# Sorting the tokens of a 32-expert FFN: one block behind an attention, or chunk by chunk within it

## The chip, the cores and the metric

The kernel runs on one core of a Trainium2 chip. The metric is the device time of one execution in microseconds (us); several executions are made and the median is taken. The core has TensorE (PE; its weight loads are listed as PEld), VectorE (DVE), ScalarE (ACT), GpSimd (POOL) and SyncE (SP, which here only issues DMAs). Each engine works through its own instructions in order.

## The reference: what is computed

A decoder of four layers over x of 128 x 64 tokens of width 128. Each layer is an attention-like block, a cross attention with a context, and an FFN, each added to x and followed by a layernorm. The change concerns layer 1, whose cross attention is causal (16 heads of width 8) and whose FFN picks one of 32 experts for each token:

```python
x = _layernorm(x + _L1_xattn_ref(x, ctx_1024, ctx_1024, ...))   # causal
x = _layernorm(x + _L1_ffn_ref(x, router_w, router_b, weights1, bias1, weights2, bias2))
```

The kernel computes that FFN as: the logits are x times the 128 x 32 router weights plus a bias; the expert with the largest logit (the first of equals) is e; y = relu(relu(x W1[e] + b1[e]) W2[e] + b2[e]), with 32 hidden units per expert.

## The kernel before

The 8192 tokens are 16 chunks of 512 (four tiles of 128). X[c] holds chunk c in SBUF throughout. The steps at the end of the kernel run one after the other: ..., attn_diff, xattn_causal, ffn_routed, attn_alibi, ....

**The attention helper** (`attention`, L1171 to L1387) is a software pipeline. Pass c does the second half of chunk c-1's values, the weights of chunk c, the scores of chunk c+1 and the projections of chunk c+2, in four parts k = 0 to 3; at the end of each it calls `aside(c, k, seen)`, with the last instructions so far (`seen`), behind which an aside can queue its own. Maxima of the scores are reductions on DVE (L1260), the exponentials run on ACT (L1309), the values are 64 small products (L1327, av_ps) and DVE normalises them (L1332, L1341). Score and weight tiles (`wide`) take turns in five PSUM banks, everything else (`bank`) in three. POOL does part of the head expansion (L1202) and applies the layernorm (L387). The causal attention passes no aside. The alibi attention behind the FFN does: its aside gathers the routed outputs back. The attention with the key mask (layer 3) does too: its aside sorts for the last FFN, mostly one chunk's transposes and logits a pass.

**The routed FFN** (`ffn_routed`, L1663) treats chunks 10 to 15 as dense and 0 to 9 as routed.

- Dense: all 32 experts at once. `choose` (L1682) transposes a chunk and makes logits and the one-hot choice, `spread` (L1691) turns the choice into a mask, `hidden` (L1702) makes 8 x 512 hidden rows in two halves of four products, a mask product and four Relus on ACT (L1714), `output` (L1717) sums over them tile by tile (L1724, L1725), and a layernorm follows. `hidden` and `output` call `between` before each half and each tile.
- Routed: `plan` (L1749) sorts the 40 tiles of 128 tokens by expert. For all ten chunks it makes transposes and logits (L1756, L1759) into one 40 x 32 table, then the one-hot choices over the whole table (DVE instructions of 1280 elements), prefix products with a triangle and with ones (L1781, L1782), counts rounded up to 128, one running sum over 1312 elements (L1793), and the positions. Then 40 indirect DMAs from POOL (L1805) write each tile's rows to their places in an array XR in HBM.
- Quads: 18 groups of four sorted tiles. `fetch` (L1818) has SP read four expert numbers and issue eight weight loads; `rows` (L1832) loads the quad's rows from XR through ACT's DMA queue (L1834); `turn` (L1836) transposes them, `inner` (L1844) and `outer` (L1852) make the two layers, and SP stores the result (L1865) from one of four buffers. `rejoined` (L1906) gathers the results within the alibi attention.

The order is written out at L1874 to L1904: the eleven logit steps of the plan, choose and spread of the first dense chunk, then the dense chunks with the rest of the plan's steps between them, `fetch` for 13 quads, three `rows`, and the quads one after the other. The plan's big tables lie in the two VX tiles and two tiles of the tag "e", which the attention uses as well. A list scheduler orders instructions at build time by readiness and by the order of tracing; `issue_after` makes it keep an instruction behind another of the same engine.

Of the kernel before, what the change touches and what calls it, by code (L numbers as in the profile page):

```python
# [12 lines left out]
F32 = mybir.dt.float32  # L13
# [227 lines left out]
def tile_decoder(ctx: ExitStack, tc: tile.TileContext, a, out):  # L241
# [1274 lines left out]
    def causal_steps():  # L1516
        w = W[4]
        return attention(
            cross(w, None, None), w[:, 2, :],
            lambda c, s: out_projected(c, s["o"], w[:, 3, :], bv=col("l1xbv"), base=lambda: with_bias(c, "l1xbo")),  # L1520
            mask=everywhere(half[:, 128:256].rearrange("p (n h k) -> p n h k", n=2, h=1)), late_laid=True,
        )
# [140 lines left out]
    def ffn_routed():  # L1663
        w = W[5]
        both, spare = work("tab", (P, 1024), "selb2"), work("tab", (P, 1024), "wqs")
# [5 lines left out]
        rest, whole = work("tmp", (P, D), "b2rest"), both[:, P : 2 * P].bitcast(BF16).rearrange("p (n m) -> p n m", n=2)  # L1671
        b2, part = whole[:, 0], whole[:, 1]
# [9 lines left out]
        def choose(c):  # L1682
            xT = transposed(X[c], "xT")
            full = (P, TPC, E32)
            l = logits(xT, col("l1fr"), E32, row("l1frb"), "lg32", work("t1", full, "lg32"))
            oh, _ = first_of(l, E32, "rev32", [P, TPC], "rt", work("tmp", full, "rt_s"), work("o", full, "rt_o"))
# [15 lines left out]
        def hidden(c, between):  # L1702
            xT, _, ohm = st[c]
            hT = work("h", (P, 8, 512), "hT8")
            for n in range(2):
# [6 lines left out]
                for j in range(4):  # L1712
                    k = 4 * n + j
                    A.activation(hT[:, k, :], ps[j], AF.Relu, bias=col("l1fb1")[:, k : k + 1])  # L1714
# [16 lines left out]
        T, NE, W_ = TPC * len(ROUTED), E32, TPC * len(ROUTED) * E32  # L1731
        span = NE * (T + 1)
        first, second = work("e", (P, 2048), "plan"), work("e", (P, 2048), "plan")
        LG, same = (t[:, :W_].rearrange("p (t e) -> p t e", t=T) for t in (first, second))
        ahead = first[:, :span].rearrange("p (e t) -> p e t", e=NE)
        inside = second[:, :W_].rearrange("p (e t) -> p e t", e=NE)
        each = VX[0][:, :span].rearrange("p (e t) -> p e t", e=NE)
        oh = VX[0][:, span : span + W_ // 2].bitcast(BF16).rearrange("p (t e) -> p t e", t=T)
        keep = VX[1][:, :span].rearrange("p (e t) -> p e t", e=NE)
        o = span  # L1740
        sums, o = VX[1][:, o : o + 4 * NE].rearrange("p (k e) -> p k e", k=4), o + 4 * NE
        halves, o = VX[1][:, o : o + P].bitcast(BF16).rearrange("p (k m) -> p k m", k=2), o + P
        pos, o = VX[1][:, o : o + T], o + T
        whole, o = VX[1][:, o : o + NE].bitcast(I32), o + NE
        whose, o = VX[1][:, o : o + P].bitcast(I32), o + P
        gf = VX[1][:, o : o + 1]
        where = RT["where"] = sm.tile([P, 40], I32, tag="pli0", name="pli", bufs=1)[:, :T]

        def plan():  # L1749
            V.tensor_copy(halves, sq[:, 1:3, :])  # L1750
            G.memset(keep, 1.0)
            G.memset(keep[:, :, 0:1], 0.0)
            behind = None
            for i in [*range(len(ROUTED)), None]:
                if i is not None:
                    xT = transposed(X[ROUTED[i]], "tmp")  # L1756
                if behind:
                    k, x = behind
                    logits(x, col("l1fr"), E32, row("l1frb"), "lg32", LG[:, k * TPC : (k + 1) * TPC, :])  # L1759
                behind = (i, xT) if i is not None else None  # L1760
                yield
            m = sm.tile([P, TMAX, 1], F32, tag="fo_m", name="p1_m")[:, :T]
            yield from first_of_steps(LG, E32, "rev32", [P, T], "rp", same, oh, m)
            V.tensor_reduce(sums[:, 0], oh.rearrange("p t e -> p e t"), AX.X, ALU.add)
            ps = bank("cnt_ps")
            mm(ps[:, :NE], sq[:, 2, :], sums[:, 0], start=True, stop=True)
            V.tensor_scalar(sums[:, 1], ps[:, :NE], float(P - 1), None, ALU.add)
            yield
            V.tensor_copy(whole, sums[:, 1])
            V.tensor_single_scalar(whole, whole, 7, ALU.logical_shift_right)  # L1770
            V.tensor_copy(sums[:, 1], whole)
            V.tensor_tensor_scan(sums[:, 2], sc("iota")[:, 1:2].to_broadcast([P, NE]), sums[:, 1], 0.0, ALU.mult, ALU.add)
            V.tensor_tensor(sums[:, 3], sums[:, 2], sums[:, 1], ALU.subtract)
            V.tensor_scalar(each[:, :, 0], sums[:, 3], float(P), None, ALU.mult)
            yield
            flat = oh.rearrange("p t e -> p (t e)")
            for k in range(0, T, 16):
                n = min(16, T - k)
                q = slice(k * NE, (k + n) * NE)
                inn, tot = wide("in_ps"), wide("tot_ps")  # L1780
                mm(inn[:, : n * NE], halves[:, 0, :], flat[:, q], start=True, stop=True)  # L1781
                mm(tot[:, : n * NE], halves[:, 1, :], flat[:, q], start=True, stop=True)  # L1782
                A.copy(inside[:, :, k : k + n], inn[:, : n * NE].rearrange("p (t e) -> p e t", t=n))
                A.copy(each[:, :, 1 + k : 1 + k + n], tot[:, : n * NE].rearrange("p (t e) -> p e t", t=n))
                yield
# [83 lines left out]
        def take(n):  # L1869
            for _ in range(n):  # L1870
                with tc.issue_after(RT["dve"].ins) if "dve" in RT else nullcontext():
                    next(planned, None)
# [427 lines left out]
```

## Time and profile before

| | us |
|---|---|
| median of 6 runs | 3144.7 (3131.98 to 3153.53) |
| the profiled execution, its time | 3152.46 |
| its span, first to last instruction | 3150.5 |
| PE busy | 2782.6 (88%) |
| DVE busy | 2008.3 (64%) |
| ACT busy | 1643.4 (52%) |
| POOL busy | 1520.8 (48%) |
| mean granted PE clock | 0.940 |

The profile records one execution. A stretch's row gives its length, each engine's busy time and the PE clock granted, as a share of the full clock. A timeline row gives start, duration, engine, line, operation, output and inputs, shapes and how many such instructions were merged; in brackets stands how long the engine idled before and on what it waited. The chain of waits follows the work that ended last back to what released it; its rows are start, duration and line. All times in the prediction count from the span's start; the causal attention's full passes lie between about 1060 and 1300, the routed FFN's stage between 1326 and 1535.

### The profile page before, as it was taken

The page shows a single profiled execution, that of the slowest core. Times are in us where ns is not written, and L with a number is a line of the kernel's source. Part 1 is how long each engine was busy: PE and PEld are TensorE (multiplying, and loading weights), DVE is VectorE, ACT ScalarE, POOL GpSimd, SP SyncE. Part 2 cuts the span into 40 slices and gives each one's busy share as a digit, 9 for nine tenths or more (in the row PEclk, how much of TensorE's full clock was granted, in tenths as well). Part 3 has the DMA queues.
Part 4 walks back from the last instruction along what each step waited for, and adds up shares of the span by engine and source line. Part 5 has one row for each costly group of instructions (what it writes and reads, how often), then busy time and mean ns, then how long its engine had stood idle before and what let it go on. Part 6 is the DMA issues. An engine that isn't in the chain of part 4 may idle for free.

```text
span 3150.5 us, 110712 instructions
## 1 busy us (share of the span) xinstructions
PE 2782.6 (88%) x46690; PEld 2046.0 (65%) x46690; DVE 2008.3 (64%) x7278; ACT 1643.4 (52%) x3376; POOL 1520.8 (48%) x1521
## 2 busy tenths in 40 slices
PE   5899989999999899998899999989898679998993
PEld 3789856656666677865577767764443347766882
DVE  3743469667777666553477656667878776674355
ACT  3444457754554565432366555644555666654453
POOL 3566556144555444325277435556666123444344
PEclk9999989999999999889899989999998889998997
DMA  4578821000000200003611000000000000011683
GB/s 129 151 202 260 253 62 43 6 8 3 3 3 7 69 4 4 7 19 99 178 19 18 4 6 4 4 12 1 1 1 11 1 12 19 17 32 61 213 254 117
DMA packets 191634, 182.23 MB, mean 58 GB/s; under 512 B 30176, under 2 KB 166624, under 8 KB 191136
## 3 DMA queue, kind: packets, MB, share of 16 engines
q1 hardware_dynamic: 160688, 136.66, 14.6%
q0 software_dynamic: 20224, 32.28, 4.2%
q8 instruction: 366, 6.00, 0.7%
q10 hardware_dynamic: 10224, 6.22, 0.7%
q14 instruction: 132, 1.08, 0.1%
HBM read 132.34 MB, written 42.73 MB: 56 GB/s over the span
## 4 chain that ended last, share of the span: by engine, by line
PE 55%; DVE 25%; POOL 5%; ACT 5%; issue 5%; DMA 4%; SPq 1%; POOLq 0%; ACTq 0%; DVEq 0%
PE av_ps L1327 9%; DVE m L1260 7%; PE s_ps L1252 5%; PE h_ps L790 5%; PE yg L803 5%; PE t_ps L1290 4%; DMA got<-l_rout,fat 2%; PE v_ps L1229 2%; PE xT_ps L332 2%; PE t_ps L1302 2%; POOL x L387 2%; PE ye_ps L2027 1%; PE y L1134 1%; PE y L1724 1%; DVE lnst L373 1%
## 5 line engine op out<-in xcount | busy, mean ns | idle before, releaser
L1260 DVE TENSOR_REDUCE m<-s_ps 128x8 f32<-128x512 f32 x640 | 397.4, 683 | 117.5 <-PE s_ps L1648 41.2
L1309 ACT ACTIVATE e<-t_ps 128x512 f32<-128x512 f32 x640 | 329.9, 602 | 150.8 <-PE t_ps L1302 150.4
L1327 PE MATMUL av_ps<-vx,e 128*64 128x18 f32 (+1 forms) x10240 | 336.4, 215 | 10.7 <-issue 5.6
L1327 PEld LDWEIGHTS av_ps<-vx,e 128*64 128x64 f32 x10240 | 318.2, 139 | 30.8 <-issue 23.1
L792 ACT ACTIVATE hT<-h_ps,aux 128x256 f32<-128x256 f32 x496 | 206.6, 469 | 221.5 <-issue 112.1
L1290 PE MATMUL t_ps<-eb,kT 32*64 32x128 f32 x10240 | 284.3, 287 | 6.9 <-DVE m L1260 2.4
L1202 POOL TENSOR_SCALAR eb<-qT,small 128x512 f32<-128x512 f32 x75 | 124.5, 1661 | 329.3 <-ACT qT L972 177.6
L825 POOL DMA_INDIRECT got<-l_rout,fat x192 | 193.7, 1009 | 174.4 <-DVE r L835 68.2
L790 PE MATMUL h_ps<-ebT,rw 128*128 128x256 f32 x992 | 242.4, 389 | 14.0 <-DVE ebT L778 8.8
L1290 PEld LDWEIGHTS t_ps<-eb,kT 32*64 32x64 f32 x10240 | 200.6, 133 | 74.6 <-DVE m L1260 25.4
L803 PEld LDWEIGHTS yg<-rw,hT 128*128 128x128 f32 x1984 | 241.0, 192 | 6.3
L803 PE MATMUL yg<-rw,hT 128*128 128x128 f32 x1984 | 241.3, 275 | 0.0
L387 POOL TENSOR_SCALAR x<-xb,lnmv,ln_y 128x128 f32<-128x128 f32 x200 | 157.2, 798 | 170.6 <-DVE ln_y L352 167.8
L1252 PE MATMUL s_ps<-eb,qT 32*64 32x256 f32 x5120 | 218.3, 399 | 16.3 <-DVE m L1260 9.7
L765 POOL DMA_INDIRECT aux<-in_x_dram,rat x156 | 159.7, 1024 | 113.3 <-PE h_ps L790 48.7
L1332 DVE RECIPROCAL rc<-av_ps 128x32 f32<-128x32 f32 (+1 forms) x192 | 61.4, 320 | 235.4 <-PE av_ps L1327 235.1
L790 PEld LDWEIGHTS h_ps<-ebT,rw 128*128 128x128 f32 x992 | 182.8, 194 | 39.2 <-DVE ebT L778 13.6
L804 DVE TENSOR_TENSOR yo<-yg,aux 128x256 f32<-128x256 f32 x124 | 52.3, 422 | 239.7 <-PE yg L803 239.5
L1200 ACT ACTIVATE eb<-qT,small 128x512 f32<-128x512 f32 x160 | 106.9, 714 | 122.6 <-POOL qT L1434 118.0
L1252 PEld LDWEIGHTS s_ps<-eb,qT 32*64 32x64 f32 x5120 | 113.8, 134 | 57.3 <-DVE m L1260 12.7
L1202 POOL TENSOR_SCALAR eb<-kT,small 128x512 f32<-128x512 f32 x75 | 136.0, 1813 | 19.3 <-ACT kT L972 10.6
L2027 PE MATMUL ye_ps<-w_l2f,box 128*128 128x512 f32 x256 | 135.2, 653 | 0.0
(525 smaller groups left out, 6381.8 us busy)
## 6 DMA issues: line engine op xcount, KB each, us to landing
rw<-in_l0w_dram SPq DMA_DIRECT2D x78, 512.0 KB
rw<-in_l3w_dram SPq DMA_DIRECT2D x46, 512.0 KB
l_rout<-yo SPq DMA_DIRECT2D x124, 128.0 KB
aux<-xd SPq DMA_DIRECT2D x46, 128.0 KB
aux<-in_l0b_dram SPq DMA_DIRECT2D x78, 66.0 KB
xd<-vx SPq DMA_DIRECT2D x5, 1024.0 KB
plan<-xr ACTq DMA_DIRECT2D x18, 256.0 KB
x<-in_x_dram SPq DMA_DIRECT2D x16, 256.0 KB
```

Source lines behind the costliest of these rows:

```text
L387: (V if on_dve else G).tensor_scalar(X[c][:, t, :], r[:, t, :], mv[:, t, 0:1], y[:, t : t + 1], ALU.subtract, ALU.mult)
L790: s.pe = mm(ps[:, j * GR : (j + 1) * GR], w1[:, (k + j) * P : (k + j + 1) * P], ebT, start=True, stop=True)
L792: s.act_ins = A.activation(hT[k + j], ps[:, j * GR : (j + 1) * GR], s.act, bias=v[:, k + j : k + j + 1])
L803: s.pe = mm(y[:, i * P : (i + 1) * P], hT[k][:, i * P : (i + 1) * P], w2[:, k, :], start=(k == 0), stop=(k == FK - 1))
L825: s.gather = G.indirect_dma_start(out=got[i][k][:, t, :], out_offset=None, in_=s.rout[b][:, :], in_offset=bass.IndirectOffsetOnAxis(ap=at[ ...
L1202: ins = (G if h == 2 and not early else V).tensor_scalar(dst, x, mine, None, ALU.mult)
L1252: mm(ps[g][j * S : (j + 1) * S, u * 256 : (u + 1) * 256].rearrange("p (h k) -> p h k", h=4), rows32(s["q"], g)[:, b], rows32(s["eb"], g)[: ...
L1260: last = V.tensor_reduce(s["m"][:, g, 2 * hf : 2 * hf + 2, :].rearrange("p t h -> p (t h)"), ps[g].rearrange("p (n k) -> p n k", k=S), AX. ...
L1290: mm(ps[g][i * S : (i + 1) * S].rearrange("p (a u j q) -> p a u j q", u=2, a=2, j=2)[:, :, u, j, :], rows32(s["k"], g)[:, b], rows32(s["eb ...
L1309: last = A.activation(e[:, g, :], ps[g], AF.Exp, scale=scale)
L1327: mm(av[j * S : (j + 1) * S, 8 * (u - u0) + n, :], ev[:, n // 2, n % 2, u, j, :], vx[:, 2 * (2 * hf + u) + j, n, :], start=True, stop=True,)
L2027: mm(ps[k].rearrange("p (e d) -> p e d", e=4), s["x1T"][n][:, t * P : (t + 1) * P], w[0][:, 4 * k : 4 * k + 4, :], start=True, stop=False, ...
```

## The change

The plan becomes a sequence of small steps for one chunk each, and it starts within the causal attention, as its aside `presort`.

- In pass c = 2 the FFN's preamble runs. From there one plan step is taken at k = 0 and k = 2 of each pass, and from (12, 3) on at every k. Chunk i's `chosen` (logits, one-hot choice, and a running count `before` of the choices per expert in the tiles ahead) is in pass i+3 at k = 0; `ranked` (two bfloat16 products of width 128 that give each token's rank among its expert's, and a product and a reduction on DVE) at k = 2 together with the transposes of the next chunk. Passes 12 and 13 make the counts, the experts' starts and the positions; passes 14 to 16 take twelve scatter steps of two tiles. `choose` and `spread` of the first dense chunk are in pass 16.
- The large tables, the running sum over 1312 elements and the copies of the prefix products go. The plan now keeps one tile of the tag "tab" and two of "t1".
- After the attention SP fetches weights for 13 quads at once. The scatter steps left are taken among the first two dense chunks, two at each `between`.
- The quads' steps are no longer behind the dense chunks: from the third chunk's output on, each `between` of `output` takes one, and from the fourth chunk on the first half of `hidden` too. Rows are loaded behind the latest Relu on ACT.

```diff
+            aside=lambda c, k, seen: presort(c, k, seen),
...
+        def turned(i):
+            st["x"] = transposed(X[ROUTED[i]], "tmp")
+
+        def chosen(i):
+            mine = oh[:, i * TPC : (i + 1) * TPC]
+            logits(st["x"], col("l1fr"), E32, row("l1frb"), "lg32", l)
+            m = sm.tile([P, TMAX, 1], F32, tag="fo_m", name="p1_m")[:, :TPC]
+            for _ in first_of_steps(l, E32, "rev32", [P, TPC], "rp", same, mine, m):
+                pass
+            for t in range(TPC):
+                z, n = divmod((i * TPC + t + 1) % (2 * TPC), TPC)
+                V.tensor_tensor(before[:, z, n], before[:, i % 2, t], mine[:, t], ALU.add)
+
+        def ranked(i):
+            q = slice(i * TPC, (i + 1) * TPC)
+            mine = oh[:, q]
+            ps = bank("rk_ps")[:, : TPC * NE]
+            mm(ps, halves[:, 0, :], mine.rearrange("p t e -> p (t e)"), start=True, stop=False)
+            mm(ps, halves[:, 1, :], before[:, i % 2].rearrange("p t e -> p (t e)"), start=False, stop=True)
+            V.tensor_tensor(same, mine, ps.rearrange("p (t e) -> p t e", t=TPC), ALU.mult)
+            V.tensor_reduce(rank[:, q], same, AX.X, ALU.add)
...
+            for i in range(n):
+                chosen(i)
                 yield
+                ranked(i)
+                if i + 1 < n:
+                    turned(i + 1)
+                yield
...
+            for k in range(0, T, 2 * TPC):
+                q = slice(k, k + 2 * TPC)
+                V.tensor_tensor(two, oh[:, q], sums[:, 0, None, :].to_broadcast([P, 2 * TPC, NE]), ALU.mult)
+                V.tensor_reduce(pos[:, : 2 * TPC], two, AX.X, ALU.add)
+                V.tensor_tensor(rank[:, q], rank[:, q], pos[:, : 2 * TPC], ALU.add)
+                if k in (0, 4 * TPC):
+                    yield
+            V.tensor_copy(where, rank)
...
+        def rows(q):
+            eb[q] = S_["first"][:, q % 4 * 512 : (q % 4 + 1) * 512].rearrange("p (i d) -> p i d", i=4)
+            with tc.issue_after(RT["act"].ins):
+                nc.scalar.dma_start(out=eb[q], in_=XR[q * 4 * P : (q + 1) * 4 * P, :].rearrange("(i p) d -> p i d", p=P))
...
+        def quads(near):
+            for q in range(3):
+                rows(q)
+            for q in range(QUADS + 2):
+                if 0 <= q - 2:
+                    outer(q - 2)
+                if q > 2 and q - 3 + near < QUADS:
+                    fetch(q - 3 + near)
+                if q + 3 < QUADS:
+                    rows(q + 3)
+                if q < QUADS:
+                    turn(q)
+                if 0 <= q - 1 < QUADS:
+                    inner(q - 1)
+                yield
...
+        def presort(c, k, seen):
+            if c < 2:
+                return
+            with ExitStack() as behind:
+                for i in seen:
+                    if i:
+                        behind.enter_context(tc.issue_after(i))
+                if k in (0, 2) or (c, k) >= (12, 3):
+                    next(planned, None)
+            if c == NC and k == 0:
+                choose(d0)
+            elif c == NC and k == 2:
+                spread(d0)
...
+        near = homes()
+        for q in range(near):
+            fetch(q)
...
-            hT = hidden(c, lambda n: take(1 if k else 0))
+            hT = hidden(c, lambda n: take(2) if k < 2 else next(quad, None) if k > 2 and n == 0 else None)
...
-            output(c, hT, lambda t: take(2 if k == t == 0 else 1 if k == 0 or t % 2 else 0))
+            output(c, hT, lambda t: take(2) if k < 2 else next(quad, None))
```

## The prediction

> **What bounds the kernel now.** I read the page's slices first: TensorE is busy 88% of the span, so the useful question is where it is idle or slow. Then the table by stretches, for the attention that the sort is moved into and for the routed FFN behind it. Columns: stretch, its length, busy time of PE, PEld, DVE, ACT and POOL with the number of instructions, granted PE clock, DMA share, GB/s.
>
> ```profile
> 1075.00:1299.00 224.00, 218.35 (x6595) 173.75 (x6580) 150.33 (x499) 133.22 (x235) 100.27 (x90) 1.00 0.02 4
> 1320.00:1356.00 36.00, 33.49 (x190) 31.31 (x189) 11.89 (x59) 7.12 (x12) 7.58 (x10) 0.54 0.03 8
> 1356.00:1458.00 102.00, 97.13 (x571) 64.87 (x570) 50.90 (x191) 35.12 (x61) 48.81 (x51) 0.98 0.17 45
> 1458.00:1474.00 16.00, 5.30 (x26) 3.67 (x25) 0.32 (x1) 2.48 (x5) 10.86 (x12) 0.65 0.34 97
> 1474.00:1496.00 22.00, 19.88 (x247) 15.73 (x249) 11.50 (x42) 5.02 (x19) 4.39 (x5) 0.95 0.51 137
> 1496.00:1536.00 40.00, 31.24 (x321) 21.00 (x314) 12.28 (x33) 9.53 (x36) 3.15 (x7) 0.62 0.69 189
> ```
>
> The causal attention (row 1) is full: PE 218 of 224 us at clock 1.00. What is put there costs about its PE time. The routed FFN has three weak stretches: planning at 0.54 of the clock, a hole of 16 us, and the quads at 0.62. The chain of waits and PE's timeline name the first two:
>
> ```profile
> 1324.13 2.08 PE y L1395 x8
> 1326.21 1.71 PE tmp_ps L332 x8
> 1330.56 1.55 PE lg_ps L453 x8
> 1333.01 1.55 PE lg_ps L453 x8
> ```
>
> ```profile
> 1459.47 1.16 PE L1724 MATMUL y<-w_l1f,hT 128*128 128x128 f32 x8
> 1471.09 0.80 PE L1724 MATMUL y<-w_l1f,hT 128*128 128x128 f32 x2 [10.46 <-ACT hT L1714]
> ```
>
> The attention's last product ends at 1326.2. Ten chunks of transposes and logits follow, 2.45 us each, with nothing beside them. At 1459 PE waits 10.46 us for an ACT Relu: the row loads of the quads (L1834) sit in ACT's queue ahead of it (one wait there lasted 10330 ns) until POOL's last scatter, issued at 1466.7, has landed. The last quad's bias products start at 1534.5 and end at 1535.1. So the stage takes 1535.1 - 1326.2 = **208.9 us**, all on the path.
>
> **The change part by part: the stage behind the attention.** Planning, the first choose and spread, and 24 of 40 scatters leave it; the quads go among dense chunks 3 to 6. I build the new stage from full-clock rows.
>
> - Dense chunks: on the chain the second half of the hidden layer starts at 1403.08, 1421.04, 1439.01: 17.97 us a chunk, 6 x 17.97 = 107.8. The last has no choose for a next one: less 0.59 (four transposes, 1276.57 to 1277.16) and 0.92 (logits, 1400.73 to 1401.65) gives 106.3.
> - Quads: from 1481.57 (hq) by 1481.93 (transposes), 1482.56, 1482.89 to the next hq at 1483.22 one takes 1.65 us of PE at full clock: 18 x 1.65 = 29.7. Each chunk's 0.84 us wait of its first output product for the Relu (2.82 us for 16 instead of 2.00) is covered by a quad's step in four chunks: -3.4.
> - Left over, my estimates: 0.2 us of new waits per step, 3.6; the last step outside the chunks, 1.5; a cold start, 2 (the first hidden layer took 4.0 us for six products at 1354, 2.7 for six at full clock); rest of the first choose in the attention's tail, which has idle spots of 1.06 and 0.78 us, 2.
>
> Sum 141.7, so the stage gets **67 us** shorter. SP: one quad's eight weight loads occupied it 5.7 us (1392.7 to 1449.6 for ten). Thirteen fetched ahead take 74 us, three of them into tiles that are free before the attention ends. The first quad's step comes some 49 us into the stage, quad 12 at about 105, so loads are in time. Output stores wait behind those fetches on SP, and there are four output buffers; I come to a near tie (store of quad 0 issued at 74, its buffer wanted at 78), nothing added; if lost, see rival C. Row loads on ACT come after chunk 2; at 1.28 us a scatter (1410.23 to 1411.61 and on) plus 3.1 us for a layernorm the 16 scatters left end about 25 us into the stage, so the 10.46 us hole goes. What is late next is PE itself. The alibi attention needs VX cleared after the last quad, as now.
>
> **The part in the causal attention.** A pass takes 16.9 us (av of one pass at 1063.01, 1079.81, 1096.72). Ten passes get, for one chunk each:
>
> - PE: logits 0.92, transposes 0.59, two bfloat16 products of width 128, about 0.1 each by the oh products (L1695): 1.7 us. The attention with the key mask does the like already (transposes and logit rows one chunk a pass): passes grow from 17.0 (2590.51 to 2607.58) to 18.6 (2660.52 to 2679.14), 1.6 for 1.6 us of PE.
> - DVE: logits' add, two reductions, three compares or products at 0.285 to 0.292 each, 1.75; four adds of 128x32 at 0.19 (L1773), 0.77; for the rank a product and a reduction, 0.58. Sum 3.1 us.
> - ACT: one copy of 0.6, into an idle spot of 2.6.
>
> The logits' 2.5 us of DVE come between the normalised output and the maxima of the next scores:
>
> ```profile
> 1279.64 0.42 DVE L1341 TENSOR_TENSOR o<-av_ps,rc 128x256 f32<-128x256 f32 x1
> 1280.71 2.48 DVE L1260 TENSOR_REDUCE m<-s_ps 128x8 f32<-128x512 f32 x4 [0.64 <-PE s_ps L1501]
> 1282.28 1.42 PE L1290 MATMUL t_ps<-eb,kT 32*64 32x128 f32 x59
> ```
>
> DVE has 0.64 us free there and gains 0.92 while PE does the logits; 2.5 do not fit. The maxima start about 1 us late, and the next weights (t_ps) need three of the four score banks freed, with almost no slack at 1282.28. I take 1.1 us per pass. The rank's 0.58 fits into the 0.8 that PE adds in its half. So 2.8 x 10 = 28. From below: only PE, less the 0.33 to 0.41 us that PE already waits for hl per pass: 1.3 x 10 = 13. From above: every DVE instruction on the path, 4.8 x 10 = 48. I take 28, nearer to the masked passes.
>
> - Counts, starts and five pairs of 128x256 product and reduction (0.43 each by the 288-wide rows at 2782.91) in passes 12 and 13, about 7 us of DVE, half of it seen: 3.5, between 0 and 8.
> - 24 scatters in passes 14 to 16: 31 us of POOL in some 45, beside 4.4 a pass for the layernorm; the expansions (1.57 and 1.85) have ended by then: 1, between 0 and 5.
> - The preamble (sel, b2) already ran at 1042 to 1049, under the attention: nothing, between -1.5 (DVE's wait for sel) and +2.5 (its own DVE time).
>
> Sum **33 us**, between about 11 and 63.
>
> **Weighed against the skill.** Between 1330 and 1338 PE was busy 8.00 of 8.00 us and the granted clock was 0.50. The Trainium skill, "TensorE: Matmul & The Clock Gate", section "What's actually happening", says that about 3.4 us of sustained activity release the full clock; this row does not agree. By the page, an estimate, ten chunks at 1.5 us (0.59 + 0.92) instead of 2.45 would have cost some 8 us less before, so the move would win 8 less.
>
> The 40 scatters took 969 to 1112 ns in the dense chunks. The Trainium skill, "SBUF — State Buffer", section "SBUF: two separate sides", speaks against the move: DVE in a two-port mode locks GpSimd out while it writes descriptors, and a transfer of about 620 ns took 3100. By that figure, an estimate, 24 scatters beside the attention's DVE work would end some 50 us later and the first row loads would hold ACT again, about 10 us more than my sum. No run here shows such a stall.
>
> **Sum.** -67 + 33 = -34 us on a profiled execution of 3152.5 us (span 3150.5). That lies 7.8 above the median shown; I take the difference off the median 3144.7: **3110 us**. A measurement tells about 0.3%, 9.4 us, from no change.
>
> **Rivals.**
> A, the forecast, 3100 to 3122: 0.52.
> B, DVE's additions hide: 10 x 1.7 + 3, -47, 3098: for it, DVE is busy only 150 of 224 us; against, the tie at 1282. 0.15.
> C, the quads are not covered: SP's 5.7 us fetches hold stores, outputs wait for buffers (as DVE and ACT now wait up to 5.1 and 4.7 us for such stores), some 22 us: -12, 3133. 0.15.
> D, slower: the added chain for the score maxima and the three shared banks makes each of the ten passes DVE-bound. In the key-mask attention one pass with several sort steps went from 2754.36 to 2782.00, 27.6 us, 10.6 over 17.0. At 8 a pass: 80 + 5 - 67 = +18, 3163; it decides from about 6.3 a pass. Against it: there steps were chained within a pass, PE waiting for ACT's copies; here a step uses what the step before left. 0.09.
> E, it does not do what it says: the steps sink to the attention's end. Then nothing is added within the passes, but planning stays exposed (10 x 2.45) and all 40 scatters come late and hold the row loads (some 30): -67 + 25 + 30 = -12, 3133. Against it: each step is issued behind instructions of its own pass. 0.09.
>
> Faster: A, B, and most of C and E, 0.83; within 0.3%: 0.08; slower, nearly all D: 0.09. The range leaves out D and the extremes: 3089 (B with 10 more from the stage) to 3138 (C and E with 5 lost).
>
> **What would show it.** Passes of the causal attention of about 19.7 us (16.9 now); DVE's maxima no longer with 0.64 idle before them; no 2.45 us pieces after the attention's last product; no wait of 10 us for L1714's Relu; clock near 1.00 from dense chunk 2 on; the stage some 142 us long. Passes over 23 us, or a stage above 175, would make the prediction wrong.

## The result, and the profile after

The changed kernel takes 3159.99 us (median of 22 runs, 3137.06 to 3175.58) against 3144.72 for the kernel before (48 runs); ratio 1.0045, 95% interval 1.003 to 1.0061. It is slower by some 14 us where a gain of 34 was forecast. Its profiled execution (3170.88 us, above the median) has a span of 3169.0 us, 18.5 above that of before, at a mean clock of 0.939.

Three stretches of each trace, cut at the same events: from the value projection's copies of pass 3 to those of pass 13 (the ten passes that get a chunk's choice), from there to the attention's last value product, from there to the last quad's products (which end at 1534.6 in the kernel before, so its row holds 0.5 us of the next step). Columns as in the prediction's tables (length; PE, PEld, DVE, ACT, POOL; clock; DMA share; GB/s). Before:

```profile
1111.53:1282.40 170.87, 166.43 (x5013) 132.58 (x5016) 113.92 (x381) 102.11 (x180) 78.03 (x71) 1.00 0.02 4
1282.40:1321.30 38.90, 37.34 (x1159) 31.32 (x1160) 22.84 (x83) 17.80 (x32) 12.00 (x12) 0.96 0.01 4
1321.30:1535.10 213.80, 185.40 (x1298) 135.00 (x1298) 85.64 (x315) 58.76 (x132) 74.78 (x84) 0.81 0.29 78
```

After:

```profile
1111.13:1336.32 225.19, 210.66 (x5144) 162.07 (x5147) 154.42 (x506) 107.39 (x190) 79.89 (x71) 0.89 0.01 3
1336.32:1377.20 40.88, 37.85 (x1159) 31.37 (x1159) 26.44 (x106) 17.80 (x32) 22.66 (x23) 0.96 0.21 49
1377.20:1544.30 167.10, 153.68 (x1167) 105.78 (x1166) 60.15 (x277) 50.22 (x113) 53.75 (x63) 0.91 0.44 122
```

The ten passes grew by 54.3 us (225.19 - 170.87), the attention's tail by 2.0, and the stage behind it shrank by 46.7 (213.80 - 167.10): +9.2 with the 0.4 by which the passes began earlier. The other 9 us of the span lie in later stages whose code is the same. There single profiles differ by chance: in the experiments below the time from the last quad to the end was between 1611 and 1629 us (1652 to 1672 on the third chip), with one unchanged 50 us stretch at a clock between 0.76 and 1.00. So the explanation rests on the ten passes and on the stage, and the verdicts rest on medians.

The row to look at first is the clock of the ten passes: 1.00 before, **0.89** after. One pass shows how. DVE, in the changed kernel (start, duration, then operation; in brackets the idle time before and its releaser):

```profile
1172.34 1.79 DVE L1759 TENSOR_TENSOR few<-few,plan 128x32 bf16<-128x32 bf16 x4
1174.05 2.48 DVE L1260 TENSOR_REDUCE m<-s_ps 128x8 f32<-128x512 f32 x4
```

TensorE, same place:

```profile
1173.43 0.43 PE L1290 MATMUL t_ps<-eb,kT 32*64 32x128 f32 x2
1174.79 0.43 PE L1290 MATMUL t_ps<-eb,kT 32*64 32x128 f32 x2 [0.93 <-DVE m L1260]
1175.38 0.43 PE L1290 MATMUL t_ps<-eb,kT 32*64 32x128 f32 x2 [0.17 <-DVE m L1260]
1175.98 1.05 PE L1290 MATMUL t_ps<-eb,kT 32*64 32x128 f32 x53 [0.17 <-DVE m L1260]
```

The maxima (L1260) stand behind the choice and the four adds; TensorE waits 0.93 + 0.17 + 0.17 = 1.27 us for score banks. That much was foreseen (1.1). What follows was not. TensorE's rows in an earlier pass (the first two) and behind that wait:

```profile
1146.33:1149.74 3.41, 3.41 (x83) 3.17 (x89) 2.54 (x14) 2.28 (x5) 1.30 (x2) 1.00 0.00 0
1149.74:1153.15 3.41, 3.41 (x52) 1.90 (x41) 3.13 (x9) 0.00 (x0) 3.10 (x4) 0.50 0.02 5
1175.00:1177.00 2.00, 1.66 (x71) 1.20 (x77) 1.52 (x3) 0.00 (x0) 0.00 (x0) 1.00 0.00 0
1177.00:1179.00 2.00, 2.00 (x69) 1.81 (x52) 0.00 (x0) 0.64 (x2) 0.00 (x0) 0.51 0.03 8
1187.00:1189.00 2.00, 2.00 (x10) 1.21 (x9) 1.96 (x5) 1.16 (x2) 0.56 (x1) 0.93 0.00 0
```

TensorE is busy 2.00 of 2.00 us, but from 1177 to 1187 at half clock: ten microseconds in which it does five microseconds' worth. The passes take 19.1 to 20.8 us where the clock holds (four of ten) and 22.5 to 26.1 where it falls.

Not every wait costs that much. The ten passes hold eight stretches at 0.50, three of 10.24 us and five of 3.41: 47.8 us, in which 23.9 us of full-clock time are lost. The changes of the clock lie whole multiples of 3.41 us apart. Seven passes have a wait of 0.92 to 0.93 us with pieces of 0.17 behind it; in five of them a stretch begins within 1.2 us of the last piece (three of 10.24, two of 3.41, together 18.8 us lost). Three passes, with waits of 0.17 us alone, are three of the four in which the clock holds. The other three stretches of 3.41 us, 5.1 us lost, follow no wait: TensorE is busy 3.41 of 3.41 us before 1149.74 (first two rows), and each of the three begins at most 0.2 us after the sort's logit products, which stand behind the value products there.

In the stage behind, the planning pieces of 2.45 us and the 10.46 us hole are gone, as foreseen. TensorE's longest waits there are new:

```profile
1406.19 1.89 PE L453 MATMUL lg_ps<-cols,xT 128*128 128x32 f32 x8 [2.56 <-DVE ohm L1702]
1421.38 0.61 PE L1698 MATMUL oh_ps<-identh,oh 128*128 128x128 bf16 x4 [4.04 <-DVE oh L1691]
1444.43 1.08 PE L1856 MATMUL ebT_ps<-ident,eb 128*128 128x128 f32 x4 [3.21 <-DMA eb<-xr]
```

The first two come from DVE. Its own waits from 1376 on (waits table: instruction, releaser, us in total, times, longest) have a line that the kernel before cannot have, since the copies L1814 are new:

```profile
DVE fat L1814 <- DMA xr<-x,fat: 26.1, 22, 4.3
```

DVE copies each scatter's offset into a ring of four small tiles and waits until a scatter has read its tile. The third wait is for the first row load, issued at 1441.64, in the same step as the transposes that need it.

### The profile page after: what moved, and what is told of

Same layout as the page of the kernel before. It is cut to its first block, busy times and chain, and to the rows that moved or that the text cites. A ratio compares the mean times of both kernels' runs of the same rounds, so it can differ in the third digit from the quotient of the medians.

```text
span 3169.0 us, 110885 instructions
## 1 busy us (share of the span) xinstructions
PE 2801.1 (88%) x46703; PEld 2051.6 (65%) x46703; DVE 2031.2 (64%) x7415; ACT 1642.2 (52%) x3370; POOL 1520.0 (48%) x1519
## 4 chain that ended last, share of the span: by engine, by line
PE 54%; DVE 27%; issue 5%; ACT 5%; DMA 5%; POOL 5%; POOLq 0%; SPq 0%; ACTq 0%; DVEq 0%
PE av_ps L1327 9%; DVE m L1260 8%; PE h_ps L790 5%; PE s_ps L1252 5%; PE yg L803 5%; PE t_ps L1290 4%; DMA got<-l_rout,fat 2%; PE y L1134 2%; PE t_ps L1302 2%; PE xT_ps L332 2%; POOL x L387 1%; PE ye_ps L2076 1%; PE y L1727 1%; PE v_ps L1229 1%; DVE lnst L373 1%
## 5 line engine op out<-in xcount | busy, mean ns | idle before, releaser
L1260 DVE TENSOR_REDUCE m<-s_ps 128x8 f32<-128x512 f32 x640 | 397.4, 683 | 117.6 <-PE s_ps L1649 42.8
L1327 PE MATMUL av_ps<-vx,e 128*64 128x18 f32 (+1 forms) x10240 | 343.9, 218 | 8.9 <-DVE o L1341 5.6
L1327 PEld LDWEIGHTS av_ps<-vx,e 128*64 128x64 f32 x10240 | 326.4, 142 | 29.0 <-issue 22.3
L1290 PE MATMUL t_ps<-eb,kT 32*64 32x128 f32 x10240 | 294.2, 287 | 16.1 <-DVE m L1260 11.4
L1202 POOL TENSOR_SCALAR eb<-kT,small 128x512 f32<-128x512 f32 x75 | 135.7, 1809 | 18.8 <-ACT kT L972 10.9
```

The costliest lines, as they stand in the source:

```text
L1202: ins = (G if h == 2 and not early else V).tensor_scalar(dst, x, mine, None, ALU.mult)
L1260: last = V.tensor_reduce(s["m"][:, g, 2 * hf : 2 * hf + 2, :].rearrange("p t h -> p (t h)"), ps[g].rearrange("p (n k) -> p n k", k=S), AX. ...
L1290: mm(ps[g][i * S : (i + 1) * S].rearrange("p (a u j q) -> p a u j q", u=2, a=2, j=2)[:, :, u, j, :], rows32(s["k"], g)[:, b], rows32(s["eb ...
L1327: mm(av[j * S : (j + 1) * S, 8 * (u - u0) + n, :], ev[:, n // 2, n % 2, u, j, :], vx[:, 2 * (2 * hf + u) + j, n, :], start=True, stop=True,)
```

## The experiments

**The theory**: in the passes, DVE's work ahead of the maxima makes TensorE wait, and the wait lets the clock fall; in the stage, DVE is tied to POOL's scatters and the first rows are asked for too late. **The rival** for the passes: the added TensorE work itself costs the clock; for the stage: POOL's scatters bound it in any case.

| kernel | ratio to before, 95% interval | ten passes, us | clock in them | TensorE's waits for the maxima: sum, longest, us | stage, us |
|---|---|---|---|---|---|
| before | 1 | 170.9 | 1.00 | 0 | 213.8 |
| after | 1.0045 (1.003 to 1.0061) | 225.2 | 0.89 | 9.0, 0.9 | 167.1 |
| e1, choice at k = 1 | 0.9942 (0.9923 to 0.9962) | 185.0 | 1.00 | 0 | 165.2 |
| e2, no copies | 1.0078 (1.005 to 1.0106) | 218.2 | | | 178.2 |
| e3, rows earlier | 1.0035 (1.0017 to 1.0054) | 217.2 | | | 160.9 |
| e4, all three | 0.9954 (0.9936 to 0.9971) | 185.2 | | | 172.2 |
| e5, own offsets | 0.9886 (0.9861 to 0.9912) | 187.1 | | | 154.7 |
| e6, adds later | 0.9963 (0.9942 to 0.9985) | 194.9 | 0.97 | 1.4, 0.2 | 167.0 |
| e7, before + 2.2 us | 1.0035 (1.001 to 1.006) | 186.3 | 1.00 | 3.4, 0.2 | |
| e8, wait filled | 1.0019 (0.9997 to 1.0041) | 213.0 | 0.98 | 1.7, 0.2 | 166.0 |
| e9, before + 3.6 us | 1.0127 (1.009 to 1.0164) | 223.2 | 0.86 | 16.7, 1.5 | |
| e12, own offsets | 0.9855 (0.9831 to 0.9879) | 186.7 | | | 154.8 |
| e13, earlier scatters | 0.9834 (0.9811 to 0.9856) | 187.1 | | | 153.3 |
| e14, quads behind | 0.9875 (0.9851 to 0.9899) | 184.9 | | | 164.3 |

The table's passes and stages are from one profile each. e1 to e4 shared a chip, e5 to e8 another, e9 to e11 a third, on which the kernel before takes 3260.2 us, e12 to e14 a fourth. Ratios are always to the kernel before on the same chip. e2 and e3 leave the ten passes as they are in the changed kernel and took 218.2 and 217.2 us for them, so 225.2 is a profile on the long side: the passes' cost is 46 to 54 us.

### e1: the choice behind the maxima

```diff
-                if k in (0, 2) or (c, k) >= (12, 3):
+                if k in (1, 2) or (c, k) >= (12, 3):
```

> Only the place of the chunk's choice changes: logits and choice are taken at k = 1 of a pass, behind the maxima of the next scores, instead of at k = 0, ahead of them; rank and next transposes stay at k = 2. Every instruction is the same. Theory 1 (the choice's 2.5 us and more on DVE delay the maxima, TensorE waits about 1.3 us for score banks, and that wait lets the granted clock fall to 0.50 for some 10 us in two of three passes): the ten passes take 18.5 to 19 us each instead of 18.5 to 26, the clock stays at 1.00 in them, and the whole gets 30 to 45 us shorter than the changed kernel: about 3120. Theory 2 (the added TensorE work itself, transposes and 32-wide products, lowers the clock, whatever DVE does): passes stay at about 22 to 25 us in most cases, and the time within 8 us of 3160.

Measured 3124.67 us. Ten passes take 185.0, nearly all 18.25 us, at a clock of 1.00. The instructions are those of the changed kernel, in number and kind; one condition moves 35 us. DVE and TensorE in one pass of it:

```profile
1144.43 2.48 DVE L1260 TENSOR_REDUCE m<-s_ps 128x8 f32<-128x512 f32 x4 [0.64 <-PE s_ps L1501]
1149.07 0.80 DVE L1759 TENSOR_TENSOR few<-few,plan 128x32 bf16<-128x32 bf16 x4
1150.93 0.36 DVE L1332 RECIPROCAL rc<-av_ps 128x32 f32<-128x32 f32 x1 [1.06 <-PE av_ps L1327]
```

```profile
1146.01 1.08 PE L453 MATMUL lg_ps<-cols,tmp 128*128 128x32 f32 x8
1147.02 1.19 PE L1290 MATMUL t_ps<-eb,kT 32*64 32x128 f32 x63
```

The maxima again have their 0.64 us of idle time before them, as in the kernel before; the choice lies in time that DVE otherwise spends waiting for the value products, and 1.06 us of that is still left. The weights (t_ps) wait for nothing. Theory 2 falls as it was put: at this place the same TensorE work costs 14.1 us in ten passes (185.0 - 170.9), 1.4 each, and no clock. But the edit moves the logit products too, away from the value products, so e1 alone doesn't tell the wait from the place of these products; e6 and e9 do.

It also prices the four adds. In the changed kernel, the durations of L1759 (min/median/max, ns):

```profile
L1759 DVE TENSOR_TENSOR few<-few,plan x40: 174/176/1167, 1109.9 to 1310.6; 128x32 bf16<-128x32 bf16 x40
```

and in e1:

```profile
L1759 DVE TENSOR_TENSOR few<-few,plan x40: 174/174/177, 1112.4 to 1277.6; 128x32 bf16<-128x32 bf16 x40
```

At k = 0 the four together take 1.79 us, at k = 1 they take 0.80. At k = 0 they run into POOL's addition L401 (in the pass above POOL works from 1172.40 to 1173.68), and one of the four is held until about its end; so it is in each of the ten passes (1154 to 1167 ns), while in e1 no addition meets L401 and none takes over 177 ns. The Trainium skill, "SBUF — State Buffer", section "Who interferes with whom", says that a DVE instruction with two SBUF inputs contends with a GpSimd instruction that reads SBUF, and that the later one blocks fully until the first is done. This trace agrees: 174 ns alone, up to 1167 beside L401.

### e2: no copies of the offsets

```diff
-                    at = sm.tile([P, 2], I32, tag="fat", name="fat", bufs=4)[:, :1]
-                    V.tensor_copy(at, where[:, n : n + 1])
...
-                        out=RT["views"][n], out_offset=bass.IndirectOffsetOnAxis(ap=at, axis=0),
+                        out=RT["views"][n], out_offset=bass.IndirectOffsetOnAxis(ap=where[:, n : n + 1], axis=0),
```

> The scatters take their offsets straight from the table of positions; the 40 copies of one column on DVE into a ring of four small tiles go. Theory (in dense chunks 0 and 1 DVE stands behind copies whose buffer a scatter still reads, and POOL issues the 40 scatters one after the other until about 1419, so that DVE is throttled to POOL's pace; chunks 0 and 1 take 23.7 and 23.5 us instead of 18): they take 18 to 19 us each, and the whole gets 8 to 12 us shorter, about 3150. Rival (POOL's scatters hold the stage in any case, since the row loads need the last of them): the wait moves to the first quads, and the gain is below 3 us.

Measured 3167.47 us, against both: slower by about 7 than the changed kernel, with a stage 11 us longer. TensorE, DVE and POOL:

```profile
1403.90 0.61 PE L1698 MATMUL oh_ps<-identh,oh 128*128 128x128 bf16 x4 [23.52 <-DVE oh L1691]
```

```profile
1400.44 0.38 DVE L375 BATCH_NORM_AGGREGATE lnmv<-lnst 128x2 f32<-128x6 f32 x4 [24.86 <-POOL x L387]
```

```profile
1396.27 0.97 POOL L1813 DMA_INDIRECT xr<-x,pli  x1 [0.30 <-issue]
1397.28 6.23 POOL L387 TENSOR_SCALAR x<-xb,lnmv,ln_y 128x128 f32<-128x128 f32 x8
```

Read them from the bottom: POOL issues scatters one after the other, from 1347.5 on with one addition between them, and only at 1397.28 two layernorm applications that were due long before; DVE's next layernorm waits for them, and TensorE for DVE. The copies did two things. Each was kept behind a DVE instruction of its step, and so each scatter came in its turn in POOL's queue. Without them nothing but the finished positions held the scatters back, and they went ahead of other work. The wait that I had blamed was real; the instruction that waited was also the one that kept the order.

### e3: the first rows a step earlier

```diff
             for q in range(3):
                 rows(q)
+            yield
...
-            hT = hidden(c, lambda n: take(2) if k < 2 else next(quad, None) if k > 2 and n == 0 else None)
+            hT = hidden(c, lambda n: take(2) if k < 2 else next(quad, None) if k > 1 and n == 0 else None)
```

> The first three row loads are taken one step earlier, at the first half of the hidden layer of dense chunk 2, instead of together with the first quad's transposes; the other steps keep their number. Theory (the first quad's transposes wait 3.2 us for rows that were asked for only 2.8 us before): that wait goes and the stage gets 3 to 5 us shorter, about 3156. Rival (an earlier row load holds ACT's queue until the last scatter has landed, as before the change): ACT's Relus of chunk 2 wait instead, and the time is the same or some us longer.

Measured 3156.81 us. The 3.21 us wait is gone from the trace and the stage is 160.9 us, 6 less. In the medians the gain is 3 us, and the two intervals overlap: as expected in size, not shown by the time alone.

### e4: the three together

> The three edits together. If each theory holds, the gains add: 35 + 10 + 4 us, so about 3110, some 1.1% below the kernel before the change. If the clock theory (theory 1) falls, about 3145, no better than before the change.

Measured 3130.38 us, no better than e1 alone: e2's edit is among the three, and its stage is 172.2 us, 7 longer than e1's. The sum failed for the reason that e2 shows; the passes kept their 185.

### e5: an own place for each offset

```diff
+        ats = plan_[:, T * NE // 2 + 2 * P :][:, :T].bitcast(I32)
...
-                    at = sm.tile([P, 2], I32, tag="fat", name="fat", bufs=4)[:, :1]
+                    at = ats[:, n : n + 1]
```

with the edits of e1 and e3.

> The choice at k = 1 and the earlier row loads as before; the 40 copies of an offset stay in DVE's order, but each has a place of its own, so that none waits until a scatter has read its buffer. POOL's order of scatters and layernorms is the same as in the changed kernel. Theory (the copies have two parts: they pin the scatters behind DVE's work, which is good, and their ring of four ties DVE to POOL's pace, which costs TensorE waits of 2.4, 2.5 and 5.5 us and the half clock behind them): dense chunks 0 and 1 take about 18 us each instead of 23, the stage falls from 165 us to about 150, and the whole to about 3110. Rival (POOL's 26 scatters still to come bound the first two dense chunks in any case): the wait moves to the row loads of the first quads, the stage stays above 160, and the time about 3120.

Measured 3117.15 us, ratio 0.9886. The copies keep the order and no longer wait; dense chunk 1 starts 17.96 us after chunk 0, where the changed kernel needs 23.75, and the stage is 154.7. The rival has a part in it, though. What is left shows in e12, the same kernel on another chip, on TensorE and on ACT:

```profile
1380.19 1.92 PE L453 MATMUL lg_ps<-cols,xT 128*128 128x32 f32 x8 [4.60 <-ACT xT L339]
```

```profile
1377.95 1.51 ACTq L1851 DMA_DIRECT2D eb<-xr  x3
1379.55 0.59 ACT L339 COPY xT<-xT_ps 128x512 f32<-128x512 f32 x1 [11.07 <-issue]
```

The three row loads sit in ACT's queue until the last scatter, issued at 1375.49, has landed, and ACT's copy behind them is late: the prediction's old hole, smaller.

### e6: only the four adds moved

```diff
+        def counted(i):
+            mine = oh[:, i * TPC : (i + 1) * TPC]
             for t in range(TPC):
...
                 chosen(i)
                 yield
+                counted(i)
+                yield
...
-                if k in (0, 2) or (c, k) >= (12, 3):
+                if k in ((0, 2) if c == 2 else (0, 1, 2)) or (c, k) >= (12, 3):
```

> The choice stays at k = 0 as in the changed kernel; only the four running-count adds are moved to k = 1, behind the maxima. DVE's work ahead of the maxima falls from about 3.5 to 1.75 us. If the length of TensorE's wait decides the clock: the wait falls from 1.3 to some 0.2 us, the clock stays near 1.00, and the time is nearly that of the kernel with the choice at k = 1, about 3125 to 3130. If any work on DVE there tips the clock: passes of 22 to 26 us remain in most of the ten, and the time is 3145 or more. The adds themselves: 0.175 us each at their new place, with none of 1.16 us, if it is POOL's addition beside them that blocks one.

Measured 3138.91 us, between the two forecasts and some 26 less than the changed kernel relative to the kernel before (0.9963 against 1.0045). The four adds were 0.77 us in my sum; taking them out of the way is worth about four fifths of what e1 gains (0.0082 of 0.0103). TensorE's waits for the maxima fall to 0.2 us at most, and the clock is 1.00 in seven of the ten passes, 0.92 in two and 0.86 in the last. The two have one stretch of 3.41 us at 0.50 each, at 1147.99 and 1243.57, 0.1 us after the sort's logit products and without a wait; the last has one of 6.83 us at a wait of 1.23 us for DVE's work on the plan's counts. So moving the adds removes what followed the waits for the maxima, and the stretches behind the logits remain.

### e7 and e9: a delay alone, in the kernel before

```diff
+    def delay(c, k, seen):
+        if k or not 3 <= c <= 12:
+            return
...
+            for _ in range(11):
+                t = sm.tile([P, 4], F32, tag="dly", name="dly", bufs=2)
+                V.tensor_reduce(t, ident.rearrange("p (t e) -> p t e", t=4), AX.X, ALU.max)
```

e9 is the same with `range(18)`.

> The kernel before, with one addition: in passes 3 to 12 of the causal attention DVE does 11 reductions of 128x128 of a constant at k = 0, about 3.2 us that nothing reads. TensorE gets no work at all. If TensorE's wait for the maxima alone lowers the clock: ten passes of 16.9 become about 18 where the clock holds and 21 to 24 where it falls to 0.50, and the time rises by 25 to 60 us. If the low activity of the sort's transposes and logits is needed as well: only the wait itself is paid, 10 x 1.3 to 1.7 us, with the clock at 1.00, and the time rises by 12 to 18 us.

The reductions followed one another every 0.20 us and not every 0.29, so the delay was 2.2 us. Measured 3161.04 us, 10.5 above the kernel before on that chip. The ten passes grew by 15.4, the clock stayed at 1.00, and TensorE's waits for the maxima came in pieces of at most 0.2 us. By my expectation that spoke for the second reading; but the wait was short of the changed kernel's, so the dose was raised.

> As the kernel before with the delay, but 18 reductions (0.20 us each by the first delay run, so 3.6 us, as much as the sort's choice takes on DVE in the changed kernel) instead of 11. TensorE gets no sort work. Theory 1a (the length of TensorE's wait decides: about 0.9 us kept the clock at 1.00, 1.3 us does not): waits of 2 us a pass, granted clock 0.8 to 0.93 in several of the ten passes, passes of up to 23 us, and the ten passes together grow by 40 us or more over the kernel before. Theory 1b (the wait together with the sort's own TensorE work, which is of low activity, is needed): the clock stays at 1.00 and only the wait is paid, ten passes grow by 22 to 30 us.

Measured 3307.61 against 3260.2 us, and ten passes of 223.2 us, as long as the changed kernel's, though TensorE has no sort work to do. On this chip e10 and e11 ran their ten passes at a clock of 1.00. One pass:

```profile
1204.99 0.43 PE L1290 MATMUL t_ps<-eb,kT 32*64 32x128 f32 x2
1206.90 0.43 PE L1290 MATMUL t_ps<-eb,kT 32*64 32x128 f32 x2 [1.48 <-DVE m L1260]
1207.50 2.38 PE L1290 MATMUL t_ps<-eb,kT 32*64 32x128 f32 x55 [0.16 <-DVE m L1260]
1211.30 3.61 PE L1327 MATMUL av_ps<-vx,e 128*64 128x18 f32 x64
```

```profile
1205.00:1207.00 2.00, 0.52 (x6) 0.28 (x4) 2.00 (x9) 1.19 (x2) 1.10 (x1) 1.00 0.03 8
1209.00:1211.00 2.00, 2.00 (x84) 1.78 (x74) 0.00 (x0) 0.00 (x0) 0.00 (x0) 0.50 0.00 0
1217.00:1219.00 2.00, 2.00 (x20) 0.72 (x5) 1.32 (x3) 0.23 (x1) 0.00 (x0) 0.89 0.00 0
```

A gap of 1.48 us, then about ten microseconds at half clock; the 64 value products take 3.61 us instead of 2.05. The wait alone is enough, though not every time: of ten waits of 1.48 or 1.49 us, one a pass, five were followed by 10.24 us at half clock, three by 3.41 us and two by none (at 1278.8 and 1299.3). That is 30.7 us lost, 3.1 a wait. The Trainium skill, "TensorE: Matmul & The Clock Gate", section "🎯 Why this matters for your kernels", warns of TensorE idle gaps above some 3 us between bursts. Here gaps of 0.92 and 1.48 us were enough in thirteen of seventeen cases, and the measurement decides.

### e8: the wait filled with work

```diff
                     next(planned, None)
+                if k == 1 and 3 <= c <= 12:
+                    ps = bank("fill_ps")
+                    for _ in range(6):
+                        mm(ps, halves[:, 1, :], half[:, 256:768], start=True, stop=True)
```

> The changed kernel with work added: in the ten passes TensorE does six bfloat16 products of 512 columns, about 1.3 us, into a bank that nothing reads, just ahead of the weights for which it otherwise waits on DVE. Theory (an idle TensorE at this point lets the clock fall): the wait is filled, the clock stays near 1.00, passes take about 20 us each, and the kernel gets 15 to 35 us faster than the changed one although it does more. Rival (the clock falls by the mean activity of the pass, or the products just come on top): no gain, or up to 13 us slower than 3160.

Measured 3156.45 us, ratio 1.0019, its interval overlapping that of the changed kernel: the time alone decides nothing, and the gain is below the 15 us I had set. The passes do show it: 213.0 us for ten instead of 225.2 with 60 more products in them, the clock at 0.98 instead of 0.89, and where the clock held in both (the first of the ten, 20.8 us) the added products cost nothing. Three stretches of 3.41 us at half clock are left; two of them, at 1150.13 and 1235.47, begin at most 0.4 us after the sort's logit products, as in e6.

### e10 and e11: inconclusive, and again as e13 and e14 beside e12

e10 and e13: positions in one step, scatters two steps at a time from the end of pass 13.

```diff
-                if k in (0, 4 * TPC):
-                    yield
...
                     next(planned, None)
+                if (c, k) >= (13, 3):
+                    next(planned, None)
```

e11 and e14: all quads behind the dense chunks.

```diff
-            hT = hidden(c, lambda n: take(2) if k < 2 else next(quad, None) if k > 1 and n == 0 else None)
+            hT = hidden(c, lambda n: take(2) if k < 2 else None)
...
-            output(c, hT, lambda t: take(2) if k < 2 else next(quad, None))
+            output(c, hT, lambda t: take(2) if k < 2 else None)
```

> The version with the choice at k = 1, earlier row loads and an own place for each offset, and in addition the positions in one step and the scatters two steps at a time from the last part of pass 13 on. Theory (POOL's 40 scatters of 1.28 us, from 1314 to 1376, are what the first row loads and so ACT's queue wait for: 4.3 us of TensorE wait at 1380): the last scatter lands 6 to 12 us earlier, that wait goes, the stage falls from 155 to about 148, the whole to about 3110. Rival (POOL's layernorms and expansions of the last attention passes are pushed back by the scatters): the last passes get longer by as much, and the time stays at 3117 or above.

> The version with the choice at k = 1 and an own place for each offset, but with the quads one after the other behind the dense chunks, as in the kernel before. So it measures what the interleaving alone is worth. Theory (prediction's step: a quad's 1.65 us of TensorE work is paid in either place, but alone the quads are held by stores, copies between the layers and a low clock, 61 us for 18 in the kernel before): the stage is 20 to 30 us longer than with quads among dense chunks (155), and the time about 3140. Rival (with 13 quads' weights fetched ahead the quads run at 1.7 to 2 us each in any case): less than 10 us longer, about 3125.

Measured 3254.77 and 3258.05 us, ratios 0.9975 (0.9951 to 0.9999) and 0.998 (0.9956 to 1.0004). The ten passes were as in e1 (184.9 and 185.4), but the attention's tail took 90 and 66 us instead of 39. TensorE of e10 there:

```profile
1415.96 0.58 PE L1290 MATMUL t_ps<-eb,kT 32*64 32x128 f32 x2 [0.77 <-issue]
1417.38 0.58 PE L1290 MATMUL t_ps<-eb,kT 32*64 32x128 f32 x2 [0.83 <-issue]
```

Two products every 1.4 us, with nothing that the profile shows to wait for, at half clock, while SP issues the quads' weight loads and POOL the scatters. That is no feature of the two edits alone, since e11 has the scatters where e5 has them and e5 on its chip had no such gaps. What TensorE lacked isn't shown. The three were therefore set side by side on one chip.

> The version with the choice at k = 1, earlier row loads and an own place for each offset, as the measure for the two beside it: about 1.1% under the kernel before on a chip where that takes 3150 us, with a stage of about 155 us.

> The same with the positions in one step and the scatters two steps at a time from the end of pass 13. If POOL's pace holds the first row loads: stage about 148 us and 5 to 8 us less than the version beside it. If the scatters push back the last passes' work on POOL, or fall on the weight loads that SP issues there: last passes longer, and no gain or a loss.

> The same with all quads behind the dense chunks. If the interleaving is worth what the prediction has it (quads alone are held by the copies between their layers, by stores and by a low clock; among dense chunks they cost 1.65 us each): stage of about 180 us, and 20 to 28 us more than the version beside it. If most of the gain came from the sort's move and the early weight loads: less than 10 us more.

Measured 3113.74, 3104.36 and 3118.62 us. **e13** has the lowest time of all: 0.9834 of the kernel before, and lower than the forecast. Its last scatter is issued at 1363.22 instead of 1375.49, and the 4.60 us wait of TensorE is gone. The medians differ by 9 us, but the stages of the two profiles by 1.5 only, and in e13's the first 15 us from 1333 on run at a clock of 0.57; the direction fits the theory, the size is not settled.

**e14**: 5 us above e12 in the median, the intervals overlapping, and 9.5 in the stage (164.3 against 154.8). This is the rival's side (below 10). Two stretches of e14 show what quads alone look like:

```profile
1440.00:1455.00 15.00, 14.28 (x159) 11.69 (x158) 7.32 (x32) 3.12 (x9) 1.96 (x3) 1.00 0.72 200
1470.00:1485.00 15.00, 11.03 (x88) 6.87 (x92) 3.94 (x9) 1.89 (x7) 0.00 (x0) 0.50 0.51 135
```

They start well, then TensorE waits for ACT's Relus between the two layers (9.7 us in six waits from 1455 on) and the clock halves; still, from the dense chunks' last product at 1447.3 to 1501.5 the 18 take 54 us. Put among dense chunks (e12) they and the wait for rows add 45 (154.8 less the 110.1 of e14's dense part). The larger part of the stage's gain comes without the interleaving, from the sort's departure and the early weight and row loads, which e14 doesn't part: with quads behind it is 213.8 - 164.3 = 49.5 of e12's 59.0.

## Why the prediction was wrong, step by step

- **"I take 1.1 us per pass"** is the step that failed. The wait itself was near: 9.0 us in the ten passes. It was priced at its own length. What it left out is the half clock. Of the 54.3 us, 14.1 are TensorE's added work (e1) and 9.0 the waits; 23.9 are lost at half clock, 18.8 of them behind the waits and 5.1 behind the logit products. The last 7.3 I can't place; e7, where the passes grew by 15.4 us at clock 1.00 with listed waits of only 3.4, shows that a delay can cost more than the waits listed. The prediction had a row with TensorE busy 8.00 of 8.00 at clock 0.50 in its hands and used it only for the planning block.
- **The four adds "at 0.19 ... 0.77"** were mis-sized: 1.79 us where they stood, since one of them is held while POOL's L401 runs. e6 takes all four out of the chain, and most of the loss goes.
- **TensorE's 1.7 us a pass** was near: 1.4.
- **The lower bound, 13 us, "only PE"**, is what e1 reaches. It took only another place in the pass. I took the place of the step as given and didn't ask where DVE has room: in the kernel before it idles up to 3.8 us at a time behind the maxima, waiting for the value products.
- **The tail, 4.5 us**: 2.0.
- **"24 scatters ... in some 45" us** failed: passes 14 to 16 hold less work, and the first scatter was issued at 1356.9, 20 us before the attention's end. Twelve were out by then, 28 were left, and POOL issued them until 1419, not for 25 us but for 42.
- **"Left over, ... 0.2 us of new waits per step"** failed for the stage: DVE's copies waited on scatters, 26.1 us in 22 waits. Chunks 0 and 1 took 23.75 and 23.55 us instead of 17.97, 11.4 us of the 20 by which the stage's saving (46.7) fell short of 67. The late first rows and the clock behind them cost some 5.7: 30.3 us for chunk 2 with four quads, 24.6 by 17.97 and four times 1.65. I counted the copies' cost as nothing, since the kernel before does without them.
- **The quads' 1.65 us** were too low: the two chunks with five quads took 27.3 and 29.6 us, 1.9 and 2.3 a quad over 17.97. SP's fetches and the output buffers, rival C, were no bound: no wait of TensorE in the stage was for a store or a weight load.
- **Rival D** named the right place, the chain to the maxima, and the wrong price. It decides "from about 6.3 a pass" only with the stage at -67; with the stage's 46.7 us it decides from about 4.2, and 5.4 was paid.

What stays open: why the clock falls behind some waits and not behind others of the same length (two of the seven of 0.92 us in the changed kernel and two of the ten of 1.48 us in e9 were not followed by it), why the same rows of logit products lower it in some passes only, and what held TensorE's products back in e10 and e11.

## What to carry to other kernels

Work moved into a full stage should be placed by the engine that has least room at that point of the pass: the same instructions cost 46 to 54 us at k = 0 and 14 at k = 1. A microsecond's gap in TensorE's work in a stretch at full clock is to be priced with the half clock behind it: here 18.8 us lost behind seven gaps of 0.92 us, some 2.7 each beside the gap, and up to some five for a single one. And before a copy or a wait is taken out, ask what order it keeps.

## What the runs showed of the hardware

- The granted clock fell to 0.50 within 1.2 us of five of seven TensorE gaps of 0.92 us (changed kernel) and of eight of ten gaps of 1.48 us (e9), for 3.41 or 10.24 us, with TensorE busy. With gaps for the maxima of at most 0.2 us it stayed at 1.00 (e7).
- It also fell for 3.41 us without a gap, at most 0.4 us after 32-wide logit products that stand behind the 64 value products: three times in the changed kernel, twice in e6, twice in e8, never in e1, where these products stand elsewhere.
- A DVE addition of two SBUF tiles, 174 ns alone, took up to 1167 ns beside POOL's addition (changed kernel).
- A scatter takes 1.28 us of POOL's queue from one to the next, beside DVE's work as well as without it (0.97 to 1.19 us each): 40 of them are 51 us of POOL.
- On one chip TensorE stood for 0.7 to 1.1 us at a time without a visible releaser while weight loads and scatters ran (e10); on another the same code didn't (e13).
